# Four graph layers on one core: moving the inversion, the divisions and the output product of the attention heads

## The chip, the cores and the metric

The kernel runs on one core of a Trainium2 chip. The metric is the device time of one execution in microseconds. A core has five engines that each work through their own queue: TensorE (PE; its weight loads are listed as PEld), VectorE (DVE), ScalarE (ACT), GpSimd (POOL) and SyncE (SP), which here only issues DMAs.

## The reference

Eight graphs (batch B = 8) share one adjacency of N = 2048 nodes with about nine edges per node; every node has 64 features. Four layers follow one another, each with `x = layernorm(x + layer(x))`:

- layer 0: one-head attention with scores `leaky_relu(s1 + s2)`
- layer 1: a softmax over neighbours, feature by feature
- layer 2: the mean over neighbours, two products, relu and a layer norm
- layer 3: four heads of dot-product attention, an output product and a second dot-product attention:

```python
h = einsum('bnc,hdc->bhnd', x, Wh)                    # 4 heads
s = where(mask, einsum('...nd,...md->...nm', h, h), NEG)
out_h = einsum('...nm,...md->...nd', softmax(s), h) + bh
z = leaky_relu(concat of the heads of out_h, 0.2)     # [B, N, 256]
h2 = z @ Wo.T                                         # [B, N, 64]
out2 = the same attention on h2, + bo; leaky_relu; layer norm
```

The change lies in the heads of layer 3, from `h` to `h2`.

## The kernel before

**Stages in the profiled execution.** Layer 0 and the building of the edge lists end at about 445 us, layer 1 at about 700, layer 2 at about 920. The heads run from there to about 1450 us, the second attention from there to the end.

**Tiles of the heads.** The nodes are cut into NT = 16 node tiles of 128. The neighbours of a tile are gathered by list: two groups of 64 nodes, five windows each, so ten gathers of 128 rows (`xs` from the DRAM table `xtab`, `fetch`, L1080). GpSimd issues them, eight ahead, into ten buffers. Two gathers make a step `j`, five steps (0 to 4) a node tile. In each step TensorE does the following for all 8 graphs and 4 heads:

- `score` (L1093), twice: the scores of gathered rows against the tile's own side `U`. ScalarE takes the exponential (L1104), VectorE multiplies by the edges (L1107, "the mask").
- `turn` (L1085): transposes the rows of the next step; ScalarE copies them out (L1088).
- a "quarter" (`QUARTERS`, L1288): a piece of work for another tile.
- `back` (L1109), twice: sums of weighted rows into PSUM (`po`, two buffers). A block of 32 nodes that is complete is copied by VectorE into `os[it]` (L1130, tile name `o`, one buffer). Row 0 of each half of `o` holds the softmax denominators.

A node tile has four such blocks, closed in steps 1, 2, 3 and 4.

**What follows the sums.** The denominators are not divided by at once. After the last block they go through DRAM: SP stores the two rows to `dtab` (L1134) and loads them as `dT` (L1136). `invert` (L1139) takes the reciprocal, stores it to `itab` (L1143), checks it (L1144, L1145), and has SP load it, broadcast to 64 partitions each, as `R` (L1150, four DMAs of 256 KB, one buffer). Meanwhile `through_w` (L1167) multiplies `o` by the head's weights: TensorE L1064, ScalarE's copy L1171, VectorE's leaky relu L1172, into `z` (two buffers). `divide` (L1174) multiplies `z` by `R` (L1176), twice. `wo_all` (L1178) is the product with Wo (L1186), copied to `hT` (L1189) and stored to `utab`. `turn_back` (L1192) transposes `hT` into `h2` (L1196), and `with_bo` (L1199) adds the bias and stores to `ktab`. `top_pieces` and `low_pieces` (L1240, L1248) split `h2` into three bf16 pieces, stored to `ptab`, and add a bias to `X`.

**Order.** Within the heads the order on TensorE, ScalarE, VectorE and GpSimd is the program's order. Only SP's is left to a scheduler. The tables at L1288 to L1290 place the work of other tiles into the steps. The second entry is the offset of the tile, so `(invert, -1)` in step 2 of tile `it` inverts the sums of tile `it - 1`:

```python
QUARTERS = [(through_w, -1, 0), (through_w, -1, 2), (sides, 1, 0), (sides, 1, 2), (wo_all, -1)]
TURNED = {0: (turn_back, -2), 2: (turn_nodes, 2)}
FIRST = {1: [(top_pieces, -2)], 2: [(invert, -1)], 3: [(low_pieces, -2)], 4: [(divide, -1, 0), (divide, -1, 2)]}
```

`TURNED` and then `FIRST` stand ahead of the step's scores; the quarter stands between turn and back. GpSimd does the additions of `with_bo` and `low_pieces` inside the loop. The last tile doesn't take the way through DRAM: `last_invert` (L1153) and the lines after the loop (L1331 on) finish it.

Of the kernel before, what the change touches and what calls it, by code (L numbers as in the profile page):

```python
# [21 lines left out]
F32 = mybir.dt.float32  # L22
# [6 lines left out]
ALU = mybir.AluOpType  # L29
# [3 lines left out]
P = 128  # L33
# [15 lines left out]
def kernel(ctx: ExitStack, tc: tile.TileContext, ins: dict, out: bass.AP):  # L49
# [644 lines left out]
    RD = 2 * HN * NP  # L694
    recT = f3w.tile([RD, P], F32, name="recT")
    few = f3w.tile([RD, NT], F32, name="few")
    early = ExitStack()
# [345 lines left out]
    with early, ExitStack() as heads:  # L1043
# [48 lines left out]
        def score(k):  # L1092
# [14 lines left out]
            nc.vector.scalar_tensor_tensor(wt, wt, 3.0e38, edge, op0=ALU.min, op1=ALU.mult)  # L1107

        def back(k):  # L1109
            it, g, s = steps[k]  # L1110
# [15 lines left out]
            for blk, a, b in blocks_of(s):  # L1126
                if s == CLOSE[blk]:
                    if (g, blk) == (0, 0):
                        os[it] = wk.tile([P, HN, NP, P], F32, name="o", bufs=1)
                    nc.vector.tensor_copy(os[it][:, :, :, node_block(g, blk)].rearrange("p h a i -> p a h i"), pos.pop((it, g, blk)))  # L1130
            if (g, s) == (NG - 1, TURN[-1]) and it < NT - 1:
                rows_of = dtab[it].rearrange("(k n) i -> k (n i)", k=2)
                for k_ in range(2):
                    nc.sync.dma_start(rows_of[k_:k_ + 1], os[it][k_ * D:k_ * D + 1].rearrange("p h a i -> p (h a i)"))  # L1134
                dTs[it] = wk.tile([2 * HN * NP, P], F32, name="dT")
                nc.sync.dma_start(dTs[it], dtab[it])  # L1136

# [77 lines left out]
        def add_head(it, h, ph):  # L1215
# [6 lines left out]
            else:  # L1222
# [4 lines left out]
                for k in range(2):  # L1227
                    nc.vector.tensor_tensor(h2[:, HB + 1 - k::2], so_far[:, HB + k::2], dst[:, HB + k::2], ALU.add)
                with_bo(it, nc.vector)

# [16 lines left out]

        def low_pieces(it, eng=nc.gpsimd):  # L1248
            hp3, rest = in_pieces.pop(it)
            nc.scalar.copy(hp3[:, 1], rest)  # L1250
            eng.tensor_tensor(hp3[:, 2], rest, hp3[:, 1], ALU.subtract)
            nc.sync.dma_start(ptab[it * P:(it + 1) * P, :], hp3.rearrange("p k n -> p (k n)"))
            eng.tensor_tensor(X[:, it], X[:, it], over(b3, [P, B, D]), ALU.add)

# [32 lines left out]

        QUARTERS = [(through_w, -1, 0), (through_w, -1, 2), (sides, 1, 0), (sides, 1, 2), (wo_all, -1)]  # L1288
        TURNED = {0: (turn_back, -2), 2: (turn_nodes, 2)}
        FIRST = {1: [(top_pieces, -2)], 2: [(invert, -1)], 3: [(low_pieces, -2)], 4: [(divide, -1, 0), (divide, -1, 2)]}  # L1290
        PER = NG * GS // 2

        engines = {mybir.EngineType.PE, mybir.EngineType.Activation, mybir.EngineType.DVE, mybir.EngineType.Pool}
        AHEAD = 8
        with tc.manual_schedule(engines=engines):
            def call(of, f, t, *a):
                if 0 <= of + t < (NT if t > 0 else NT - 1):
                    f(of + t, *a)
# [8 lines left out]
            for m in range(len(steps) // 2):  # L1307
# [22 lines left out]

            t = NT - 1  # L1331
            through_w(t, 0)
            through_w(t, 2)
# [7 lines left out]
            for it in (t - 1, t):  # L1341
                top_pieces(it)
                low_pieces(it, nc.vector)

    with ExitStack() as fifth:
# [181 lines left out]
        def look():  # L1527
            many_recs(8, last_recs)
            nc.vector.memset(nbad[:, 9:10], 0.0)
            nc.vector.tensor_reduce(nbad[0:RD, 9:10], few[:, 0:NT - 1], AX.X, ALU.add)  # L1530
            nc.vector.tensor_scalar(nbad[0:RD, 9:10], nbad[0:RD, 9:10], float((NT - 1) * P), None, op0=ALU.not_equal)
            lack = fp.tile([P, 5, NT], F32, name="lack")
# [624 lines left out]
```

## Time and profile before

| what | us |
|---|---|
| median of 3 runs | 1844.16 |
| lowest and highest of them | 1836.62, 1847.84 |
| the profiled execution | 1753.84 |
| its span, first to last instruction | 1752.0 |
| TensorE busy in the span | 1326.0 (76%) |
| VectorE busy | 1219.1 (70%) |
| ScalarE busy | 910.7 (52%) |
| GpSimd busy | 830.5 (47%) |
| mean granted TensorE clock | 0.870 |

How to read it: all durations below come from the one profiled execution, which took less than the timed runs. A line of a profile names the source line, the engine, the operation, and the tiles as out<-in. A bracket at the end of a line is the engine's idle time just before, and what ended it. The clock is the share of TensorE's full clock that was granted. Busy time of an engine that isn't the bound of its stage costs nothing.

### The profile page before, as it was taken

The numbers are of one execution on the slowest core, as the hardware profiler recorded it, in microseconds if no ns is written. First come the engines' busy times: TensorE is split into PE (matmuls) and PEld (weight loads), VectorE is DVE, ScalarE is ACT, GpSimd is POOL, SyncE is SP. The second block draws the span as 40 slices with busy tenths as digits, with TensorE's granted clock in tenths as the row PEclk, the third lists the DMA queues.
The fourth block names the chain that finished last, engine by engine and source line by source line (L and its number), as shares of the span: only waits on it lengthen the run. The fifth ranks groups of instructions, "written<-read, shape, count | busy, mean of one in ns | idle before, by whom it ended". The sixth has DMA issues, their size and how long they took to land.

```text
span 1752.0 us, 39984 instructions
## 1 busy us (share of the span) xinstructions
PE 1326.0 (76%) x16028; PEld 923.5 (53%) x16028; DVE 1219.1 (70%) x2931; ACT 910.7 (52%) x1863; POOL 830.5 (47%) x820
## 2 busy tenths in 40 slices
PE   4674355552689996898947878889789787999993
PEld 3663233321233332732217767777677675888783
DVE  5889479897676465665774666766667654787787
ACT  5763234645951232535654546555556443477674
POOL 0000576670564652666625334434444316677761
PEclk9755567776799998999878999999999997999997
DMA  6451566661226883256614565654645527687771
GB/s 186 167 168 49 158 203 192 190 200 33 92 99 217 320 309 127 86 158 187 188 52 136 134 160 145 156 155 135 161 135 144 155 73 239 181 235 214 216 213 45
DMA packets 154139, 280.71 MB, mean 160 GB/s; under 512 B 64892, under 2 KB 91452, under 8 KB 151868
## 3 DMA queue, kind: packets, MB, share of 16 engines
q0 software_dynamic: 56320, 189.44, 36.2%
q1 hardware_dynamic: 80986, 84.45, 16.3%
q10 hardware_dynamic: 16640, 4.20, 1.1%
q8 instruction: 128, 2.10, 0.5%
q14 instruction: 65, 0.53, 0.1%
HBM read 237.60 MB, written 40.42 MB: 159 GB/s over the span
## 4 chain that ended last, share of the span: by engine, by line
PE 30%; DVE 15%; DMA 10%; ACT 7%; issue 4%; POOL 2%; SPq 2%; DVEq 0%; ACTq 0%; POOLq 0%
DMA R<-itab 6%; PE pa L605 6%; PE pscore L1101 3%; PE po L1123 3%; PE pa L660 3%; PE ps L1413 2%; DVE w L1107 2%; PE pscore L1186 2%; DMA itab<-rT 2%; PE po L1452 2%; PE py L833 2%; SPq L1150 2%; PE pt L1390 1%; PE pa L1003 1%; ACT z L870 1%
## 5 line engine op out<-in xcount | busy, mean ns | idle before, releaser
L204 POOL DMA_INDIRECT xs<-xtab,src x160 | 166.3, 1039 | 269.7 <-PE po L1123 238.2
L204 POOL DMA_INDIRECT hs<-htab,src x160 | 153.7, 960 | 240.4 <-PE pe L455 181.8
L1107 DVE SCALAR_TENSOR_TENSOR w<-w,Sel 128x640 f32<-128x640 f32 (+2 forms) x160 | 174.3, 1125 | 83.9 <-ACT w L1104 83.7
L605 PE MATMUL pa<-R,ET 128*128 128x512 bf16 x768 | 179.9, 391 | 50.3 <-POOL R L593 34.7
L1104 ACT ACTIVATE w<-pscore 128x640 f32<-128x640 f32 (+2 forms) x160 | 119.4, 747 | 135.4 <-PE pscore L1101 128.1
L204 POOL DMA_INDIRECT hs<-ktab,src x160 | 158.0, 987 | 60.6 <-issue 36.3
L1101 PE MATMUL pscore<-U,xsT 64*128 64x80 f32 (+2 forms) x2560 | 161.9, 277 | 1.1 <-ACT xsT L1088 1.1
L170 ACT ACTIVATE X<-X,ln_m,ln_r 128x64 f32<-128x64 f32 x256 | 87.2, 428 | 144.7 <-DVE ln_m L162 144.7
L605 PEld LDWEIGHTS <-ET 128*128 128x128 fp8e4 x768 | 74.8, 100 | 163.3 <-issue 83.5
L1123 PE MATMUL po<-w,xs 128*64 128x88 f32 (+2 forms) x3072 | 131.0, 239 | 31.3 <-DVE w L1107 30.1
L1101 PEld LDWEIGHTS pscore<-U,xsT 64*128 64x128 f32 x2560 | 150.9, 190 | 5.5 <-ACT xsT L1088 1.3
L1123 PEld LDWEIGHTS po<-w,xs 128*64 128x64 f32 x3072 | 114.5, 141 | 69.8 <-DVE w L1107 58.7
L204 POOL DMA_INDIRECT rs<-rtab,src x80 | 76.1, 951 | 62.5 <-PE pa L660 42.8
L614 DVE RECIPROCAL rec<-pa 128x256 f32<-128x256 f32 x32 | 54.1, 1730 | 64.2 <-PE pa L660 38.0
L1413 PE MATMUL ps<-U,hsT 128*128 128x64 f32 x768 | 95.5, 271 | 1.5 <-ACT hsT L1391 1.5
L1413 PEld LDWEIGHTS ps<-U,hsT 128*128 128x128 f32 x768 | 94.2, 195 | 1.9 <-ACT hsT L1391 1.7
L476 DVE TENSOR_TENSOR hs<-hs,w 128x1024 f32<-128x1024 f32 x80 | 91.8, 1214 | 3.3 <-ACT w L465 3.3
L1500 ACT ACTIVATE z<-z,ln_m,ln_r 128x64 f32<-128x64 f32 x240 | 83.5, 431 | 15.4 <-DVE ln_m L1488 15.4
L1003 PE MATMUL pa<-Y,ET 128*128 128x512 bf16 x384 | 90.1, 384 | 0.0
L204 POOL DMA_INDIRECT rs<-ytab,src x80 | 77.4, 968 | 24.0 <-issue 15.3
L1088 ACT COPY xsT<-pt 128x1024 f32<-128x1024 f32 x80 | 80.5, 1007 | 10.0 <-PE pt L713 9.9
L1452 PE MATMUL po<-hs,w 128*32 128x65 f32 x2048 | 72.9, 225 | 7.7 <-DVE w L1425 7.7
(637 smaller groups left out, 3029.5 us busy)
## 6 DMA issues: line engine op xcount, KB each, us to landing
at<-in_adj SPq DMA_DIRECT2D x16, 1024.0 KB
R<-itab SPq DMA_DIRECT2D x60, 256.0 KB
rtab<-r SPq DMA_DIRECT2D x16, 512.0 KB
ptab<-hp SPq DMA_DIRECT2D x16, 384.0 KB
hi<-ptab SPq DMA_DIRECT2D x16, 384.0 KB
ktab<-hb SPq DMA_DIRECT2D x16, 260.0 KB
X<-in_x ACTq DMA_DIRECT2D x16, 256.0 KB
htab<-H SPq DMA_DIRECT2D x16, 256.0 KB
```

The lines of the kernel that those rows point to most:

```text
L170: nc.scalar.activation(v[:, b], v[:, b], AF.Identity, scale=rstd[:, k:k + 1], bias=nmr[:, k:k + 1])
L204: nc.gpsimd.indirect_dma_start(out=dst, out_offset=None, in_=table[:, :], in_offset=bass.IndirectOffsetOnAxis(ap=src[:, it, s, g:g + 1], a ...
L476: nc.vector.tensor_tensor(wx, wx, along(w[:, own].rearrange("p g b -> p (g b)")), ALU.mult)
L605: nc.tensor.matmul(po[h].rearrange("p a f -> p (a f)"), ET[:, jt, it * P:(it + 1) * P], R[:, jt, q, h].rearrange("p a f -> p (a f)"), star ...
L1003: nc.tensor.matmul(sums[it], ET[:, jt, it * P:(it + 1) * P], Y[:, jt, q].rearrange("p a n -> p (a n)"), start=(jt == 0 and q == 0), stop=( ...
L1101: nc.tensor.matmul(pscore[:, k_, f0:f0 + HN * ni].rearrange("p (h i) -> p h i", i=ni), xsT[half, p], Us[it][half, p, :, i0:i0 + ni], start ...
L1104: nc.scalar.activation(w.rearrange("p k a h i -> p k (a h i)"), pscore[:, :, 0:NP * HN * ni], AF.Exp)
L1107: nc.vector.scalar_tensor_tensor(wt, wt, 3.0e38, edge, op0=ALU.min, op1=ALU.mult)
L1123: nc.tensor.matmul(po[half, p, :, a - blk * GB:b - blk * GB], xs[:, f0:f0 + D], w[:, k_, p, :, a - WINDOWS[s][0]:b - WINDOWS[s][0]], start ...
L1413: nc.tensor.matmul(pscore[:, g, 2 * p:2 * p + 2], hsT[:, g, p], U[:, p, :, node_block(g, k)], start=False, stop=(p == NP - 1))
L1452: nc.tensor.matmul(po[node_block(g, k), j, b], w[:, g, t], hs[:, g, t], start=(s == BEGIN[k] and b == 0), stop=(s == END[k] and b == B // ...
L1500: nc.scalar.activation(v, v, AF.Identity, scale=r, bias=n)
```

## The change

The work of the heads is placed anew, in four respects.

- **The inversion.** `dT`, `rT` and the check's tiles are 128 partitions x 32 instead of 32 x 128. The same 4096 numbers are read and stored row by row in DRAM order (`spread`). `invert` moves from ahead of step 2's scores to behind step 1's turn.
- **Divisions and Wo.** `divide` and `wo_all` move from step 4 of the next tile to step 0 of the tile after that. What precedes and follows shifts by a step: `through_w` to steps 1 and 2, `turn_back` to 1, `top_pieces` to 2, `turn_nodes` to 3, `low_pieces` to 4, `sides` to 3 and 4. After the loop, the divisions and Wo of tile 14 are added.
- **GpSimd.** The additions of `with_bo` and `low_pieces` run on VectorE. `with_bo` reads the PSUM tile of the transposes instead of `h2`. `low_pieces` gives its ScalarE copy to a new `middle_piece`, behind step 3's turn.
- **First block's copy.** The copy of the first block of sums into `o` moves from step 1's back to behind step 2's turn (`out_of_sums`).

```diff
-    recT = f3w.tile([RD, P], F32, name="recT")
-    few = f3w.tile([RD, NT], F32, name="few")
+    recT = f3w.tile([P, RD], F32, name="recT")
+    few = f3w.tile([P, NT], F32, name="few")
...
+        def out_of_sums(it, g, blk):
+            nc.vector.tensor_copy(os[it][:, :, :, node_block(g, blk)].rearrange("p h a i -> p a h i"), pos.pop((it, g, blk)))
...
                     if (g, blk) == (0, 0):
                         os[it] = wk.tile([P, HN, NP, P], F32, name="o", bufs=1)
-                    nc.vector.tensor_copy(os[it][:, :, :, node_block(g, blk)].rearrange("p h a i -> p a h i"), pos.pop((it, g, blk)))
+                    if (g, blk) != (0, 0):
+                        out_of_sums(it, g, blk)
...
-                dTs[it] = wk.tile([2 * HN * NP, P], F32, name="dT")
-                nc.sync.dma_start(dTs[it], dtab[it])
+                dTs[it] = wk.tile([P, RD], F32, name="dT")
+                nc.sync.dma_start(dTs[it], spread(dtab[it]))
+
+        def spread(rows_of):
+            return rows_of.rearrange("r i -> (r i)").rearrange("(p c) -> p c", c=RD)
...
-            rT = wk.tile([RD, P], F32, name="rT")
+            rT = wk.tile([P, RD], F32, name="rT")
             nc.vector.reciprocal(rT, dT)
-            nc.sync.dma_start(itab[it], rT)
+            nc.sync.dma_start(spread(itab[it]), rT)
...
-            with_bo(it, nc.gpsimd)
-
-        def with_bo(it, eng):
+            with_bo(it, ph[:, :, 0].rearrange("p k a d -> p a k d"))
+
+        def with_bo(it, v):
             hb = hbs[it % 2]
-            eng.tensor_tensor(hb[:, :, 1:1 + P].rearrange("p a (k d) -> p a k d", d=D), h2s[it].rearrange("p (a k) d -> p a k d", k=2),
-                              over(bo, [P, NP, 2, D]), ALU.add)
+            nc.vector.tensor_tensor(hb[:, :, 1:1 + P].rearrange("p a (k d) -> p a k d", d=D), v, over(bo, [P, NP, 2, D]), ALU.add)
...
-        def low_pieces(it, eng=nc.gpsimd):
+        def middle_piece(it):
+            hp3, rest = in_pieces[it]
+            nc.scalar.copy(hp3[:, 1], rest)
+
+        def low_pieces(it):
             hp3, rest = in_pieces.pop(it)
-            nc.scalar.copy(hp3[:, 1], rest)
-            eng.tensor_tensor(hp3[:, 2], rest, hp3[:, 1], ALU.subtract)
+            nc.vector.tensor_tensor(hp3[:, 2], rest, hp3[:, 1], ALU.subtract)
             nc.sync.dma_start(ptab[it * P:(it + 1) * P, :], hp3.rearrange("p k n -> p (k n)"))
-            eng.tensor_tensor(X[:, it], X[:, it], over(b3, [P, B, D]), ALU.add)
+            nc.vector.tensor_tensor(X[:, it], X[:, it], over(b3, [P, B, D]), ALU.add)
...
-        QUARTERS = [(through_w, -1, 0), (through_w, -1, 2), (sides, 1, 0), (sides, 1, 2), (wo_all, -1)]
-        TURNED = {0: (turn_back, -2), 2: (turn_nodes, 2)}
-        FIRST = {1: [(top_pieces, -2)], 2: [(invert, -1)], 3: [(low_pieces, -2)], 4: [(divide, -1, 0), (divide, -1, 2)]}
+        QUARTERS = [(wo_all, -2), (through_w, -1, 0), (through_w, -1, 2), (sides, 1, 0), (sides, 1, 2)]
+        TURNED = {1: (turn_back, -2), 3: (turn_nodes, 2)}
+        BEFORE = {0: [(divide, -2, 0), (divide, -2, 2)], 2: [(top_pieces, -2)], 4: [(low_pieces, -2)]}
+        BEHIND = {1: [(invert, -1)], 2: [(out_of_sums, 0, 0, 0)], 3: [(middle_piece, -2)]}
...
-                for of in FIRST.get(j, ()):
+                for of in BEFORE.get(j, ()):
                     call(it, *of)
                 for k in two:
                     score(k)
                 if 2 * m + 2 < len(steps):
                     turn((2 * m + 2, 2 * m + 3))
+                for of in BEHIND.get(j, ()):
+                    call(it, *of)
                 call(it, *QUARTERS[j])
...
             t = NT - 1
+            divide(t - 1, 0)
+            divide(t - 1, 2)
+            wo_all(t - 1)
             through_w(t, 0)
             through_w(t, 2)
```

The remaining lines fit the check of the inverted sums at the end of the kernel to the new shape.

More of the change, by code (lines that the diff above doesn't have):

```diff
@@ L1228, in add_head @@
                     nc.vector.tensor_tensor(h2[:, HB + 1 - k::2], so_far[:, HB + k::2], dst[:, HB + k::2], ALU.add)
-                with_bo(it, nc.vector)
+                with_bo(it, h2.rearrange("p (a k) d -> p a k d", k=2))
         def turn_last(it):
@@ L1296, in call @@
             def call(of, f, t, *a):
-                if 0 <= of + t < (NT if t > 0 else NT - 1):
+                if 0 <= of + t < (NT if t >= 0 else NT - 1):
                     f(of + t, *a)
@@ L1342 @@
                 top_pieces(it)
-                low_pieces(it, nc.vector)
+                middle_piece(it)
+                low_pieces(it)
     with ExitStack() as fifth:
@@ L1528, in look @@
             many_recs(8, last_recs)
-            nc.vector.memset(nbad[:, 9:10], 0.0)
-            nc.vector.tensor_reduce(nbad[0:RD, 9:10], few[:, 0:NT - 1], AX.X, ALU.add)
-            nc.vector.tensor_scalar(nbad[0:RD, 9:10], nbad[0:RD, 9:10], float((NT - 1) * P), None, op0=ALU.not_equal)
+            nc.vector.tensor_reduce(nbad[:, 9:10], few[:, 0:NT - 1], AX.X, ALU.add)
+            nc.vector.tensor_scalar(nbad[:, 9:10], nbad[:, 9:10], float((NT - 1) * RD), None, op0=ALU.not_equal)
             lack = fp.tile([P, 5, NT], F32, name="lack")
```

## The prediction

> **What bounds the kernel now.** I read the page's chain of work first, because a change in one stage can only pay there.
>
> ```profile
> PE 30%; DVE 15%; DMA 10%; ACT 7%; issue 4%; POOL 2%; SPq 2%; DVEq 0%; ACTq 0%; POOLq 0%
> DMA R<-itab 6%; PE pa L605 6%; PE pscore L1101 3%; PE po L1123 3%; PE pa L660 3%; PE ps L1413 2%; DVE w L1107 2%; PE pscore L1186 2%; DMA itab<-rT 2%; PE po L1452 2%; PE py L833 2%; SPq L1150 2%; PE pt L1390 1%; PE pa L1003 1%; ACT z L870 1%
> ```
>
> The load of the inverted sums, `R<-itab`, its store and its issue make 10% of the chain, and all three belong to the heads. Next come the waits inside the heads (window 970 to 1420 us; us in total, times, longest), first TensorE's, then VectorE's.
>
> ```profile
> PE pscore L1186 <- DVE z L1176: 33.8, 13, 4.5
> PE po L1123 <- DVE w L1107: 28.4, 39, 1.7
> ...
> DVE w L1107 <- ACT w L1104: 56.1, 42, 1.7
> DVE z L1176 <- DMA R<-itab: 40.1, 14, 4.8
> ```
>
> TensorE waits for two things: for the divided `z` before Wo (L1186), which waits for R, and for the masks (L1107). Third, the timeline of TensorE in part of one node tile shows where these waits stand.
>
> ```profile
> 1099.68 2.02 PE L1101 MATMUL pscore<-U,xsT 64*128 64x96 f32 x32
> 1101.54 0.66 PE L713 MATMUL pt<-ident,xs 64*128 64x64 f32 x16
> 1102.12 1.09 PE L1064 MATMUL pscore<-xT,G 64*64 64x256 f32 x16
> 1104.87 1.76 PE L1123 MATMUL po<-w,xs 128*64 128x48 f32 x48 [1.65 <-DVE w L1107]
> 1106.56 2.02 PE L1101 MATMUL pscore<-U,xsT 64*128 64x80 f32 x32
> 1108.42 0.66 PE L713 MATMUL pt<-ident,xs 64*128 64x64 f32 x16
> 1110.59 1.71 PE L1186 MATMUL pscore<-z,WoT 64*64 64x256 f32 x24 [1.51 <-DVE z L1176]
> ```
>
> Apart from these two waits TensorE runs without a gap: it is the bound, and the waits are what can be won. Fourth, why the masks are late, in the same timeline and in a tile where GpSimd has finished.
>
> ```profile
> 1070.76 1.17 POOL L1251 TENSOR_TENSOR hp<-rest,hp 128x512 bf16<-128x512 f32 x1
> 1070.86 3.91 DVE L1107 SCALAR_TENSOR_TENSOR w<-w,Sel 128x768 f32<-128x768 f32 x2 [1.58 <-ACT w L1104]
> 1071.88 1.27 POOL L1253 TENSOR_TENSOR X<-X,b 128x512 f32<-128x512 f32 x1
> ...
> 1421.94 1.76 DVE L1107 SCALAR_TENSOR_TENSOR w<-w,Sel 128x768 f32<-128x768 f32 x2 [1.90 <-ACT w L1104]
> ```
>
> The same two masks take 3.91 us beside GpSimd's two operations and 1.76 us without. Last, two node tiles by windows (from one L1142 to the next; length, busy time of PE, PEld, DVE, ACT, POOL, then clock, DMA share, GB/s), and all fourteen together.
>
> ```profile
> 1095.88:1126.32 30.44, 26.75 (x548) 22.45 (x548) 21.88 (x27) 17.83 (x25) 14.30 (x14) 1.00 0.57 155
> 1254.94:1289.74 34.80, 28.84 (x548) 23.85 (x548) 21.88 (x26) 17.83 (x25) 14.30 (x14) 0.90 0.53 136
> 967.21:1416.11 448.90, 385.37 (x7610) 321.82 (x7610) 303.04 (x352) 248.31 (x336) 191.86 (x177) 0.97 0.55 146
> ```
>
> The first tile waited 1.85 us for R, the second 4.12 us. It is 4.36 us longer for 2.27 us more of waiting: the clock fell after the wait, and TensorE's work took 28.84 instead of 26.75 us. The mean tile is 448.90 / 14 = 32.06 us.
>
> **What the skill says.** "SBUF — State Buffer", section "Who interferes with whom": a VectorE instruction with two SBUF inputs contends with a GpSimd instruction that reads SBUF, and the second to issue blocks. The mask has two SBUF inputs; the 3.91 against 1.76 us agree. "TensorE: Matmul & The Clock Gate", Part 1: TensorE falls to half clock after an idle window of about 3.4 us. The trace agrees in kind: each wait of 3.5 to 4.9 us for R is followed by a 5 us stretch at 0.50 to 0.82, while most waits near 2 us leave 1.00. "VectorE: DVE Perf Modes", section "Why PSUM operands drop a tier": PSUM input limits fp32 to one element a cycle. For an fp32 `tensor_tensor` the trace shows no difference: 691 ns from PSUM (L1217) and 683 ns from SBUF (L1253 on VectorE). "DMA: Bandwidth & Descriptors", Specifications: under 512 B the DMA engine does a read-modify-write; the change makes the rows of dT and itab 128 B. No run here shows such a pair.
>
> **Part by part, for one node tile.** A clean step on TensorE is scores 2.0, turn about 0.5 after overlap, a quarter 1.1 and back 1.4 to 1.75 us. VectorE's two masks end about 3.8 us after the step's scores begin.
>
> *Inversion.* `reciprocal` on 32 x 128 takes 930 ns. The 128 x 256 one (L614) takes 1730, so 800 ns more for 128 more elements, 6.25 ns each; 32 elements then cost about 930 - 96 x 6.25 = 330 ns. The two checks fall from 215 and 280 to an estimated 115 and 180. VectorE gets about 0.8 us back. The group also moves from ahead of step 2's masks to behind step 1's; the 0.20 us that TensorE waits in step 2 goes. Its input: dT is issued 3.5 us after the tile's first scores (1087.29 against 1083.77), and the inversion falls due at about 6.4 + 0.4 + 3.8 = 10.6 us, so the trip has 7 us. The itab store of the same size took 2.2 to 3.5 us on the chain. Doubling it for 128 B rows still fits: cost 0, at the other end 0.5 us.
>
> *Division and Wo.* In the fourteen full tiles R let the divisions start 12.2 to 14.7 us after the reciprocal's end. From 11 us after the new tile's start to the divisions 0.8 us into the next tile are some 17 us. So the wait for R goes, with SP's issue of the four loads and the ptab store behind them no longer near anyone. What is late next: the divisions (2 x 1.22 us) stand ahead of step 0's masks and behind the last copy of sums, 0.1 to 0.8 us. They end at 3.2 us. Wo's first half may start at 2.5, when turn ends, and needs the first `z` (2.0); its second half starts at 3.6. The masks end at 4.05 and 5.0 us; back starts at 4.7, and its second part at 5.3. Cost 0; 0.4 us if the queue slips. Their old cover was R itself, so nothing is lost in step 4.
>
> *GpSimd's arithmetic.* Three operations of 1.29, 1.17 and 1.27 us leave GpSimd; three of 0.69 us join VectorE. The masks win back 3.91 - 1.76 = 2.15 us and 2.68 - 1.62 = 1.06 us. VectorE's sum: 21.88 - 3.2 - 0.8 + 2.1 = 20.0 us in a tile of 27: not the bound. TensorE's 1.65 us goes, and about 0.3 us of step 0. `with_bo` now reads the transposes' PSUM buffer, which the next turn needs 2 us later: ready at about 1.3, cost 0. The subtraction and the addition before step 4's masks delay the first of them by 0.3 us, which the quarter hides.
>
> *First copy of sums.* It leaves step 1 and stands behind step 2's masks. The single buffer `o` is still read by `through_w` there, which ends 3.6 us into the step; the copy (0.68 us) then ends at about 4.5. Back's second part needs the PSUM buffer that it frees and could start at 4.25. Cost 0.3 to 0.4 us; ends 0 and 1.2 (if VectorE comes late from the leaky step, which ends 0.7 us into step 2, and the top piece behind it).
>
> *The tail.* Wo and the divisions of tile 14 now run after the loop: `through_w` starts about 3.4 us later after the last back, and 2.14 + 1.25 us leave step 4. Cost 0, between -2 and 2.
>
> *Sum.* 30.44 - 1.65 - 1.51 - 0.3 - 0.2 = 26.8, which is TensorE's busy 26.75; with 0.4 of the copy and 0.2 for slips 27.4 us. That is 4.66 below the mean tile: 3.0 are the clean tile's and 1.6 the longer waits and the clock's. 14 x 4.66 = 65, and the last tile's mask wait of 1.5 us may go too, which I leave as reserve. The ends: 27.0 us gives 71, 28.8 us gives 46. The profiled execution took 1753.84 us (span 1752.0), so 1689. The median of the runs shown is 1844.16, 90 us above it, and no view says where these lie. I carry the difference over as it is: 1844 - 65 = 1779. If the heads stretch with the rest the gain rises 5%, to 68; if their TensorE work is slower, R waits less and the gain falls towards 50.
>
> **Rivals.**
> *VectorE's queue becomes the limit.* For: the slack ahead of the masks is 0.1 to 0.6 us in steps 0, 2 and 4. Against: 20 us busy in 27. At 0.4 us more in each of five steps the tile is 29.4: 14 x 2.66 = 37, so 1807.
> *The relief doesn't come.* R is late again by about 2 us, because its 1 MB meets the gathers (the DMA share already stands at 1.0 there) in a shorter tile. Against: 3 us of slack. TensorE's wait for z returns in step 0 and holds the masks too: about 31 us a tile, 14 x 1 = 14, so 1830.
> *Slower: the trip of the sums.* dtab's write and dT's 128 B reads take 12 us instead of 7. Then the reciprocal blocks VectorE with leaky, the top piece, step 2's masks and the copy behind it, and TensorE idles about 4.5 us; with the clock's 2.1 us that is 6.6 against 4.66 gained: 14 x 1.94 = 27, so 1871. It decides from 2.6 us of gap (7 + 0.5 + 2.6, about 10 us of trip). Against: 16 KB only, and no sign of a wait for dT today.
>
> **How the numbers follow.** The forecast has 0.64 (own range 1768 to 1798), VectorE 0.18, no relief 0.08, slower 0.10. A measurement here tells about 1% from no change. Forecast and VectorE give faster by over 1%, 0.82; no relief gives within 1%, 0.08; the last 0.10 slower. The range reaches from 1762 (71 us and the 5%, with the last tile's reserve) to 1822, which takes in VectorE's case.
>
> **What would show it.** No DVE wait for R in the heads; L1107's 768-wide pair near 1.8 us everywhere; tiles of 27 to 28 us at clock 1.00; R's DMA gone from the chain. TensorE waits of over 1 us behind the copy of sums or the divisions point to the VectorE rival, a wait of the reciprocal on dT to the slower one. A tile above 31 us makes the forecast wrong.

## The result and the profile after

| comparison | kernel before | changed kernel | ratio, 95% interval |
|---|---|---|---|
| of the result | 1846.0 us (4 runs) | 1815.9 us (4 runs) | 0.9847, 0.9801 to 0.9894 |
| again, group B | 1848.6 us (17 runs) | 1831.7 us (5 runs) | 0.9914, 0.9897 to 0.9930 |
| again, group A | 1746.6 us (11 runs) | 1678.2 us (6 runs) | 0.9601, 0.9568 to 0.9634 |

The change is faster, by 30 us where 65 were forecast. The kernels of one comparison ran on the same chip, and the comparisons fall into two groups by the time of the kernel before: about 1750 us (A below) and about 1848 us (B). The profile that the prediction read, 1753.84 us, is of group A; the times it was to be held against are of group B. The later comparisons ran on five chips, two that gave A and three that gave B; none was met twice, and that of the result isn't on record. So whether A and B are kinds of chips or conditions that one chip can be in isn't shown. The changed kernel gains 68 us in A and 17 and 30 us in B.

The changed kernel in the comparison of the result (span 1808.8 us, group B), the page's chain of work:

```profile
PE 48%; ACT 8%; DVE 7%; issue 5%; DMA 1%; another core or an unknown queue 1%; POOL 1%; SPq 0%; ACTq 0%; POOLq 0%; DVEq 0%
PE pscore L1101 9%; PE pa L605 6%; PE po L1126 5%; PE ps L1429 5%; PE po L1468 4%; PE pt L1406 3%; PE pa L660 2%; PE pt L713 2%; ACT w L1104 2%; PE pa L1003 2%; PE pscore L1064 2%; PE py L833 2%; PE pe L1399 2%; PE pscore L1193 2%; ACT xsT L1088 1%
```

DMA went from 10% of the chain to 1%: R's load, store and issue are gone from it. The waits inside the heads (window 980 to 1440 us; us in total, times, longest):

```profile
PE pscore L1064 <- ACT w L1104: 13.3, 32, 0.6
PE po L1126 <- ACT z L1178: 5.0, 10, 0.5
...
PE pscore L1193 <- DVE z L1183: 2.0, 1, 2.0
```

TensorE no longer waits for the divided `z`, except once behind the loop, and its waits for the masks have shrunk to 2.6 us in 4 (longest 1.1). What is left are many small waits for ScalarE, which head the list here and don't appear in the list that the prediction read (in group B the kernel before has them too, see below). Next, all fourteen intervals between reciprocals (length, busy time of PE, PEld, DVE, ACT, POOL, clock, DMA share, GB/s): the changed kernel of the result, then the changed kernel in A, the kernel before in A and the kernel before in B.

```profile
998.60:1408.50 409.90, 380.54 (x7612) 319.22 (x7611) 278.33 (x392) 242.35 (x336) 151.78 (x138) 1.00 0.61 160
```

```profile
962.90:1337.40 374.50, 368.31 (x7614) 314.51 (x7614) 279.76 (x392) 248.25 (x336) 154.38 (x138) 1.00 0.67 175
```

```profile
965.80:1415.60 449.80, 386.55 (x7614) 322.67 (x7610) 302.79 (x353) 248.40 (x336) 191.08 (x177) 0.97 0.55 146
```

```profile
1012.70:1456.20 443.50, 394.54 (x7604) 327.61 (x7604) 272.36 (x352) 242.17 (x336) 185.14 (x177) 0.97 0.57 148
```

Divided by 14, a tile of the changed kernel takes 29.28 us in the result's run and 26.75 in A; a tile of the kernel before 32.13 in A and 31.68 in B. The tiles of the kernel before lose nothing when it goes from A to B; those of the changed kernel lose 2.5 us each (3.2 in the other run in B). Of these 2.5 us, 1.7 are idle time of TensorE and 0.9 recorded busy time (27.2 for 26.3 us a tile); the single matmuls are recorded as equally long (scores 275 ns in both), and the granted clock is 1.00 in both. The whole heads, from the first gather of `xs` to the first gather of the fifth stage, in us:

| | before, A | changed, A | before, B | changed, B (result) | changed, B (again) |
|---|---|---|---|---|---|
| to the first reciprocal | 44.1 | 41.7 | 53.4 | 50.6 | 52.4 |
| 14 tiles | 449.8 | 374.5 | 443.5 | 409.9 | 419.4 |
| from the last reciprocal | 35.2 | 37.8 | 34.9 | 39.0 | 40.7 |
| heads | 529.1 | 454.0 | 531.8 | 499.5 | 512.5 |
| fifth stage, to the end | 302.0 | 298.9 | 364.8 | 361.3 | 359.6 |

The reciprocal itself moved: it starts 9.7 us after its tile's first scores in the changed kernel in A, and 11.9 before. So some 2 us pass from the first row to the last without being won or lost. Counted from the last tile's first scores, the end of the heads takes 47.3 us before and 47.6 after in A, and 47.3, 48.8 and 51.0 in B.

The spans of the kernel before differ by 103 us between the groups: 26 to the last gather of layer 0, 11 from there to the heads, 3 in the heads and 63 in the fifth stage. Outside the heads the changed kernel differs by much the same (23 to 26, 4 to 9 and 61 to 62 us), so none of that is the change's.

### The profile page after: what moved, and what is told of

It is laid out like the page before. It is cut to its first block, busy times and chain, and to the rows that moved or that the text cites. A ratio compares the mean times of both kernels' runs of the same rounds, so it can differ in the third digit from the quotient of the medians.

```text
span 1808.8 us, 39940 instructions
## 1 busy us (share of the span) xinstructions
PE 1378.3 (76%) x16028; PEld 949.9 (53%) x16028; DVE 1195.8 (66%) x2973; ACT 905.6 (50%) x1863; POOL 782.8 (43%) x777
## 4 chain that ended last, share of the span: by engine, by line
PE 48%; ACT 8%; DVE 7%; issue 5%; DMA 1%; another core or an unknown queue 1%; POOL 1%; SPq 0%; ACTq 0%; POOLq 0%; DVEq 0%
PE pscore L1101 9%; PE pa L605 6%; PE po L1126 5%; PE ps L1429 5%; PE po L1468 4%; PE pt L1406 3%; PE pa L660 2%; PE pt L713 2%; ACT w L1104 2%; PE pa L1003 2%; PE pscore L1064 2%; PE py L833 2%; PE pe L1399 2%; PE pscore L1193 2%; ACT xsT L1088 1%
## 5 line engine op out<-in xcount | busy, mean ns | idle before, releaser
L204 POOL DMA_INDIRECT xs<-xtab,src x160 | 172.9, 1081 | 282.0 <-PE po L1126 243.9
L1107 DVE SCALAR_TENSOR_TENSOR w<-w,Sel 128x640 f32<-128x640 f32 (+2 forms) x160 | 134.2, 875 | 104.7 <-ACT w L1104 104.5
L1104 ACT ACTIVATE w<-pscore 128x640 f32<-128x640 f32 (+2 forms) x160 | 113.6, 745 | 145.5 <-PE pscore L1101 139.9
L1468 PE MATMUL po<-hs,w 128*32 128x65 f32 x2048 | 87.3, 234 | 33.2 <-issue 25.3
L1429 PE MATMUL ps<-U,hsT 128*128 128x64 f32 x768 | 104.3, 287 | 9.0 <-ACT hsT L1407 4.8
L1429 PEld LDWEIGHTS ps<-U,hsT 128*128 128x128 f32 x768 | 102.8, 210 | 10.0 <-ACT hsT L1407 5.4
L1468 PEld LDWEIGHTS po<-hs,w 128*32 128x32 f32 x2048 | 70.8, 118 | 45.0 <-issue 33.4
L1407 ACT COPY hsT<-pt 128x512 f32<-128x512 f32 x96 | 52.5, 586 | 81.8 <-remote 46.4
```

The source lines that it names most:

```text
L204: nc.gpsimd.indirect_dma_start(out=dst, out_offset=None, in_=table[:, :], in_offset=bass.IndirectOffsetOnAxis(ap=src[:, it, s, g:g + 1], a ...
L1104: nc.scalar.activation(w.rearrange("p k a h i -> p k (a h i)"), pscore[:, :, 0:NP * HN * ni], AF.Exp)
L1429: nc.tensor.matmul(pscore[:, g, 2 * p:2 * p + 2], hsT[:, g, p], U[:, p, :, node_block(g, k)], start=False, stop=(p == NP - 1))
L1468: nc.tensor.matmul(po[node_block(g, k), j, b], w[:, g, t], hs[:, g, t], start=(s == BEGIN[k] and b == 0), stop=(s == END[k] and b == B // ...
```

## The experiments

Below, a tile is the mean of the fourteen intervals between reciprocals. Two theories were held against each other. *V*: VectorE's arithmetic ahead of the masks (top_pieces in step 2, low_pieces in step 4) holds up exponentials and masks. *T*: TensorE is later than its records show.

**The kernel before, three more times.** No edit.

> The kernel before, unchanged, for a second profile. The first profiled execution (1753.84 us) lies 92 us under the median of its timed runs (1846), and in it layer 0 took 445 us against 466 after and the fifth stage 297 against 358, in code that the change doesn't touch. If that is the execution and not the kernel, this profile spans about 1840 us, with layer 0 near 465 and the fifth stage near 350, and the heads from the first gather to the first gather of the fifth stage at 528 us as before. If the change has lengthened the other stages, layer 0 and the fifth stage are again near 445 and 297.

> The kernel before, for its profile beside the run of the changed kernel on the same chip. Where it takes about 1848: theory T expects TensorE's semaphores late against its recorded ends there too (in some 40% of the updates in the heads, as in the three kernels profiled so), a tile of about 32 us, since the waits for R give TensorE time to catch up, layer 0 near 466 and the fifth stage near 355. Where it takes about 1750: as in the second profile, 32.1 a tile, layer 0 at 444, the fifth stage at 301, no late semaphores.

> The kernel before, for a profile where it takes about 1848 us. Theory T (TensorE's late updates cost every kernel there, and the waits for R hide part of them in the kernel before): updates late in 30 to 45% of the cases in its heads too, but the step that waits for R no longer than elsewhere; a tile of 31.5 to 33 us, so that the change gains 2 us a tile there and not 5; layer 0 near 466 us and the fifth stage near 355. If the late updates belonged to the order of the changed kernel: no late updates in its heads. Where it takes about 1750: as in the profiles before, 31.9 to 32.1 a tile.

The first two met group A: 1755.96 and 1754.57 us, tiles of 32.31 and 32.13 us, layer 0 and the fifth stage as in the first profile. The third met group B: 1857.7 us, a tile of 31.68 us. So the long layer 0 and fifth stage belong to the group and not to the change. The waits of the kernel before in A (window 990 to 1400 us), TensorE's and VectorE's:

```profile
PE pscore L1186 <- DVE z L1176: 29.4, 12, 4.1
PE po L1123 <- DVE w L1107: 26.3, 36, 1.7
...
DVE z L1176 <- DMA R<-itab: 35.2, 13, 4.4
```

and in B (window 1030 to 1440 us):

```profile
PE pscore L1064 <- ACT w L1104: 13.4, 34, 0.6
PE pt L713 <- issue: 11.5, 43, 0.5
PE po L1123 <- DVE w L1107: 6.2, 13, 0.7
PE pscore L1186 <- DVE z L1176: 5.6, 5, 1.5
...
DVE z L1176 <- DMA R<-itab: 9.7, 6, 2.5
```

This is the core of the case. In thirteen tiles VectorE waited 35.2 us for R in A, and 9.7 us in B; TensorE waited 29.4 us for the divided `z` in A, and 5.6 us in B. The waits that the change removes were for the most part not there in B. They were covered by a longer way to them: from scores to scores, in the mean of fourteen tiles, steps 0, 2 and 3 were 0.4, 0.5 and 0.4 us longer in B, step 4 was 1.7 us shorter (7.91 for 9.58). In their place stand waits for ScalarE's exponentials, and 11.5 us of short gaps before turns for which the profile names nothing ("issue").

**The changed kernel, twice more.** No edit.

> The changed kernel, unchanged, a second time. With its pieces moved behind the masks it ran at 1687 us beside a kernel before of 1751, and the result of 1816 stood beside a kernel before of 1846: the two comparisons had different times for the same kernel before. Theory C (what was 92 us longer in the comparison of the result is that run's condition, the same for both kernels in kind and not caused by the change): where the kernel before takes about 1750 us here, layer 0 takes 445 us again, a tile of heads 27.2 to 27.6 and the whole 1685 to 1695, a ratio of 0.963 to 0.968. Theory V (the pieces ahead of the masks are what cost the missing 2 us a tile): a tile of 28.5 to 29.3, the whole 1705 to 1718, a ratio of 0.974 to 0.981, whatever the condition.

> The changed kernel, unchanged, a third time, for the missing pair: so far it was only timed where the kernel before takes 1846 to 1849 us (there a tile of heads of 29.3 and 30.0 us), and the forecast rests on a profile of the kernel before at 1754. Where the kernel before takes about 1750: theory T (what the kernels lose where the kernel before takes 1846 is TensorE's, whose semaphores there come later than the ends in its records) expects a tile of 27.2 to 27.6 us, the whole at 1685 to 1695, a ratio of 0.963 to 0.968; theory V (the pieces ahead of the masks) a tile of 28.5 or more, 1705 or more. Where the kernel before takes about 1848 again: a tile of 29.3 to 30.1 and a ratio of 0.983 to 0.992 by both.

The first met B: 1831.7 us and 29.96 us a tile. Theory V was to hold there too, at 28.5 to 29.3 and a ratio of 0.974 to 0.981; it got 0.9914. The second met A: 1678.2 us, a ratio of 0.9601 and 26.75 us a tile, with nine of fifteen tiles, from scores to scores, at 26.53 to 26.58 us. That is theory T's side, and somewhat better than its 27.2 to 27.6. TensorE's waits in A (window 980 to 1320 us) are

```profile
PE pscore L1101 <- issue: 0.9, 1, 0.9
PE po L1126 <- issue: 0.8, 1, 0.8
```

and nothing else: it runs through, busy 368.31 of 374.50 us. Where B differs is seen in the timeline of step 2 of one tile, first in A, then in B (start, length, engine; in brackets the idle time before):

```profile
1097.86 2.02 PE L1101 MATMUL pscore<-U,xsT 64*128 64x88 f32 x32
...
1099.04 1.59 ACT L1104 ACTIVATE w<-pscore 128x704 f32<-128x704 f32 x2 [0.82 <-PE pscore L1101]
...
1100.30 1.09 PE L1064 MATMUL pscore<-o,AT 64*64 64x256 f32 x16
```

```profile
1158.32 2.02 PE L1101 MATMUL pscore<-U,xsT 64*128 64x88 f32 x32
...
1161.00 1.35 ACT L1104 ACTIVATE w<-pscore 128x704 f32<-128x704 f32 x2 [2.18 <-PE pscore L1101]
1161.79 0.89 DVE L1107 SCALAR_TENSOR_TENSOR w<-w,Sel 128x704 f32<-128x704 f32 x1 [1.62 <-ACT w L1104]
1161.81 0.88 PE L1064 MATMUL pscore<-o,AT 64*64 64x256 f32 x12 [0.46 <-ACT w L1104]
```

The scores have the same recorded length, 2.02 us. The first exponential starts 1.18 us after them in A and 2.68 us after them in B, where ScalarE stood idle for 2.18 us. The quarter's matmuls need the buffer that the exponential reads; they start 2.44 us after the scores in A and 3.49 in B. What ScalarE waited for is TensorE's semaphore, the counter by which one engine's result releases another engine. The Trainium skill, "Perfetto Trace Analysis", section "Tensor Engine Instruction (MATMUL, LD_WEIGHTS)", says that TensorE's end in a profile is estimated, and that the semaphore update comes when PSUM has acknowledged the writes. The trace has both, and here they part. Worked out from the semaphore events, update minus recorded end, in us:

```
step 2, changed kernel     14 tiles, A   14 tiles, B (again)
scores, first half             0.02        1.50 to 1.72
scores, second half            0.02        0.77 to 1.00
next turn                  0.01 to 0.02    0.01 to 0.20
quarter                        0.04            0.04

updates over 0.15 us late, in the fourteen tiles
A: before 0 of 444, changed 0 of 445
B: before 41%, changed 42% (result) and 43% (again)
```

In the result's run the first half's update is 1.40 to 1.73 us late in ten of fourteen tiles and about 0.75 in the other four. VectorE's and ScalarE's updates are on time in both groups (medians 0.01 us, none over 0.15), and their durations are the same (the 704-wide mask 891 ns in A, 889 in B). The gathers are no slower either: one of their packets takes 159 ns in the median in both. So it is TensorE's, and it is of the group and not of the change. It is not simply a slower array: in B an update that was 1.5 us late is followed by the next, of 16 further matmuls, 0.16 us later in most tiles (0.89 in A), and the one after that is nearly on time. What holds these updates back stays open. All nine profiles of A have no late update in the tiles, all eleven of B have 37 to 45%. Nor is it peculiar to the heads: in the three profiles of B above, 13% of TensorE's updates are late in layer 0 and 18 to 59% in the later stages, in A at most three of some 1180 in the whole program. In the waits of the fifth stage the profile has a name of its own for a semaphore that comes long after the recorded end (changed kernel in B, window 1468 to 1827 us):

```profile
ACT hsT L1407 <- remote: 42.5, 9, 5.6
...
ACT w L1432 <- remote: 27.7, 12, 10.6
```

In A neither line appears.

**The pieces behind the masks.**

```diff
-BEFORE = {0: [...], 2: [(top_pieces, -2)], 4: [(low_pieces, -2)]}
-BEHIND = {1: [(invert, -1)], 2: [(out_of_sums, 0, 0, 0)], 3: [(middle_piece, -2)]}
+BEFORE = {0: [...]}
+BEHIND = {1: [(invert, -1)], 2: [(out_of_sums, 0, 0, 0), (top_pieces, -2)], 3: [(middle_piece, -2)], 4: [(low_pieces, -2)]}
```

> The changed kernel, with top_pieces and low_pieces called behind the masks and the next turn (in BEHIND) and no longer ahead of the scores of steps 2 and 4. In the changed kernel a tile of heads takes 29.28 us where 27.4 was forecast, and steps 2 and 4 are each about 1 us too long; in just these steps the first exponentials begin 2 to 2.5 us after the first score and 0.2 us after the end of rest or of X + b3. Theory V (VectorE's arithmetic ahead of the masks holds up the exponentials and masks): the tile falls to about 27.5 us, the total by about 25 us to 1791. Theory T (TensorE's own work is longer than its records show, and the exponentials are late because the scores are): nothing moves, tile 29.0 to 29.5, total within 5 us of 1816.

> The changed kernel with top_pieces and low_pieces behind the masks, again. Where the kernel before takes 1848, theory T: TensorE is the floor there, the tile stays at 29.3 to 30.1 us and the whole within 8 us of the changed kernel's. Theory V: 27.5 to 28.5 and some 25 us less than the changed kernel. Where the kernel before takes 1750: 27.2 and 1687 again, and the difference to the changed kernel beside it is what the place of the pieces is worth: theory T within 6 us, theory V 20 to 30.

Both met A: 1687.2 and 1686.1 us (ratios 0.9643, 0.9598 to 0.9689, and 0.9651, 0.9610 to 0.9693), tiles of 27.44 and 27.41 us. When the first came in it looked like a success of theory V, since only the 29.28 of group B was known; beside the changed kernel in A (26.75) it is 0.66 us a tile worse. Its one repeated TensorE wait says why (window 1000 to 1330 us):

```profile
PE pscore L1101 <- DVE U L1074: 8.4, 11, 0.8
```

Behind step 4's masks, low_pieces delays the copy of U, for which the next tile's scores wait 0.8 us. Theory V fell in A: ahead of the masks is the better place there. This kernel was not met in B.

**Bfloat16 in the quarters.** The operands are read as the upper halves of the float32 values.

```diff
-nc.tensor.matmul(pq[to, j, n]..., W[own, h, own], v(h)[own, 2 * j:2 * j + 2]..., ...)
+nc.tensor.matmul(pq[to, j, n]..., W[own, h, own].bitcast(BF16)[:, 1::2], v(h)[own, 2 * j:2 * j + 2]....bitcast(BF16)[:, 1::2], ...)
```

> The changed kernel, with the matmuls of quarters (sides and through_w, 64 of a tile's about 550) reading the upper halves of their float32 operands as bfloat16: the low bits are left out. The other engines' instructions are the same. The records give these matmuls 61.5 us in 14 tiles, 4.4 us a tile; [...] TensorE has about 3 us a tile less to do. Theory T: TensorE is the floor, and the tile falls by 2 to 3 us, to 26.3 to 27.3, the total to about 1780. Theory V: TensorE has room already; the tile stays above 28.7 us.

> The changed kernel with the operands of quarters read as the upper halves of their float32 values (the low bits are left out), again: about 3 us a tile less for TensorE, nothing less for the others. Where the kernel before takes 1848, theory T: the tile falls from 30.0 to 26.5 to 28 us. A limit that is not TensorE's execution (instructions arriving, VectorE, DMA): 29 us or more. Where the kernel before takes 1750: 25.65 and 1666 again; the difference to the changed kernel beside it says how far TensorE is the floor there: 1.5 us or more a tile if the changed kernel is at 27.2, 3 or more if it is at 28.7.

> The changed kernel with the operands of quarters read as the upper halves of their float32 values (the low bits are left out). On the other chip it took 25.65 us a tile for 26.53. Where the kernel before takes 1848: if the late updates are TensorE working off more than it can, less work makes them fewer and the tile falls by 1 us or more from 30.0, to 29 or less; if they come late whatever it has to do, the tile stays between 29.3 and 30.1. Where the kernel before takes 1750: 25.7 again.

In A twice: 1665.8 and 1668.6 us (0.9531 and 0.9547), tiles of 25.81 and 25.89 us. A quarter before (as of the changed kernel in A) and after, both from the timeline of TensorE:

```profile
1095.53 1.09 PE L1064 MATMUL pscore<-o,AT 64*64 64x256 f32 x16
1096.55 1.38 PE L1126 MATMUL po<-w,xs 128*64 128x88 f32 x32
```

```profile
1098.83 0.42 PE L1064 MATMUL pscore<-o,AT 64*64 64x256 bf16 x8
1099.31 0.83 PE L1126 MATMUL po<-w,xs 128*64 128x88 f32 x16
1100.76 0.78 PE L1126 MATMUL po<-w,xs 128*64 128x80 f32 x16 [0.63 <-DVE o L1110]
```

From the quarter's start to the start of back it is 1.02 us in float32 and 0.48 in bfloat16 (half of the bfloat16 records are missing, so starts are compared and not busy times): 0.54 us less in each of four quarters, 2.2 us a tile where about 3 were expected. The tile fell by 0.9 only. TensorE was the floor in A, but by less than 1 us: with less to do it waits for masks and for the copy of sums (8.4 and 7.5 us in a window of 320 us). In B: 1826.6 us (0.9839, 0.9792 to 0.9886), a tile of 29.43 us for 29.96, but after the first tile ten of fourteen lie between 27.5 and 29.3 and three at 31.4 to 31.8 us. Each of these three has a stretch of 6.8 us at half the clock (0.89 in the window of the tile), the others have none. Updates over 0.15 us late fell from 43% to 37%. A microsecond was asked for and half of one came in the mean, but 1.2 in the eleven tiles at full clock (28.7 us after the first tile, for 29.9 in the changed kernel). This leaves undecided how far the late updates depend on TensorE's load.

**GpSimd's additions back on GpSimd**, in the places of the change.

```diff
-            with_bo(it, ph[:, :, 0].rearrange("p k a d -> p a k d"))
+            with_bo(it, h2s[it].rearrange("p (a k) d -> p a k d", k=2), nc.gpsimd)
-            nc.vector.tensor_tensor(hp3[:, 2], rest, hp3[:, 1], ALU.subtract)
-            nc.vector.tensor_tensor(X[:, it], X[:, it], over(b3, [P, B, D]), ALU.add)
+            nc.gpsimd.tensor_tensor(...)   # both
```

> The changed kernel, with the three additions that it took from GpSimd (h2 + bo, the third piece, X + b3) back on GpSimd, h2 + bo reading the copy in SBUF; the places in the order are those of the change. Theory V: VectorE has 2 us a tile less ahead of its masks but the masks beside GpSimd's additions take longer again, 2.15 us for steps 1 and 4 by the profile before: tile between 28.3 and 29.8 us. Theory T: the masks have room, tile 29.0 to 29.6, total within 6 us of 1816. The prediction's own sum (shorter masks are worth about a microsecond and more a tile): tile 30.3 or more, total about 1831.

In A: 1705.2 us (0.9747, 0.9700 to 0.9794), a tile of 28.76 us. Against the changed kernel in A that is 2.0 us a tile, or 28 us of the change's 75 in the heads; some 6 of the 28 lie in two tiles with a stretch of low clock, and the most frequent tile is 28.38 us for 26.53. The masks in this kernel (window 990 to 1350 us), then in the changed kernel in A (980 to 1320 us); columns: busy, mean ns, idle before:

```profile
L1107 DVE SCALAR_TENSOR_TENSOR w<-w,Sel 128x640 f32<-128x640 f32 x50 | 67.9, 1358 | 12.4 <-ACT w L1104 12.4
L1107 DVE SCALAR_TENSOR_TENSOR w<-w,Sel 128x704 f32<-128x704 f32 x51 | 52.2, 1024 | 51.7 <-ACT w L1104 51.7
```

```profile
L1107 DVE SCALAR_TENSOR_TENSOR w<-w,Sel 128x704 f32<-128x704 f32 x50 | 44.6, 891 | 9.5 <-ACT w L1104 8.9
L1107 DVE SCALAR_TENSOR_TENSOR w<-w,Sel 128x640 f32<-128x640 f32 x51 | 42.0, 823 | 1.0 <-ACT w L1104 0.9
...
L1107 DVE SCALAR_TENSOR_TENSOR w<-w,Sel 128x768 f32<-128x768 f32 x26 | 24.9, 956 | 12.1 <-ACT w L1104 12.1
```

The same masks take 1358 and 1024 ns in the mean with GpSimd's additions and 823 and 891 without, four of each kind in a tile: 2.7 us of VectorE's time. With R out of the way TensorE waits for masks again, 17.0 us in 12 waits, and step 4 is 1.3 us longer than the changed kernel's (6.47 for 5.13).

**One part at a time.** The inversion alone in the kernel before (tables spread over 128 partitions, as in the change's diff), three times:

```diff
-FIRST = {1: [(top_pieces, -2)], 2: [(invert, -1)], 3: ...
+FIRST = {1: [(top_pieces, -2)], 3: ...
+                if j == 1:
+                    call(it, invert, -1)      # behind score and turn
```

> The kernel before with the first part of the change alone: the sums inverted on 128 partitions, called behind step 1's masks and not ahead of step 2's scores; divisions, Wo and GpSimd's additions where they were. If R's trip is what holds the tile, an issue some 4 to 5 us sooner takes most of the long wait for R in step 4 (3.5 to 4.9 us) away: a tile of 28.5 to 30 us for 32.1. If the sums' trip to dT becomes late (the rival on the slower side), VectorE waits for dT in step 1 and the tile stays at 31 or more.

> The kernel before with the first part of the change alone (sums inverted on 128 partitions, behind step 1's masks). Where the kernel before takes 1848 it had 30.0 us a tile, as the whole change. Where it takes 1750: R some 5 us sooner; theory R (the wait for R is all that a tile loses, 3.5 to 4.9 us): 27.5 to 28.6 us a tile, a ratio of 0.966 to 0.975; if masks beside GpSimd's additions are the next limit, as the change with the additions back on GpSimd (28.38) suggests, 28.4 to 29.5.

> The kernel before with the first part alone (sums inverted on 128 partitions, behind step 1's masks), for the chip where the kernel before takes 1747 us. If the wait for R is all that a tile loses beside GpSimd's additions: 27.5 to 28.6 us a tile, a ratio of 0.966 to 0.975. If masks beside GpSimd's additions are the next limit, as the change with the additions back on GpSimd (28.38) suggests: 28.4 to 29.5. Where the kernel before takes 1848: 30.0 again.

The changed kernel with the inversion as it was, on 32 partitions (the expectations say 16, which is a slip) and in step 2, three times:

```diff
-BEFORE = {..., 2: [(top_pieces, -2)], ...}
-BEHIND = {1: [(invert, -1)], 2: ...}
+BEFORE = {..., 2: [(invert, -1), (top_pieces, -2)], ...}
+BEHIND = {2: ...}
```

> The changed kernel with the inversion as it was: on 16 partitions, reciprocal and checks of 930 + 215 + 280 ns, ahead of step 2's scores. Divisions and Wo stay in the next tile's step 0, so R has the time of steps 2, 3 and 4, some 16 us, for a trip that had about 13 before. R is not waited for; only VectorE's 0.8 us more remain, ahead of step 2's masks. If the moved division alone frees the path: a tile within 0.8 us of the changed kernel's on the same chip. If the inversion on 128 partitions is needed too: 1.5 us or more above it.

> The changed kernel with the inversion on 16 partitions and ahead of step 2's scores, as it was. Where the kernel before takes 1848 it had 30.0 us a tile, as the whole change. Where it takes 1750: if the moved divisions alone free the path, a tile of 26.5 to 27.3 us, within 0.8 us of the change; if the sooner inversion is needed too, 27.5 or more, and a wait for R in step 0.

> The changed kernel with the inversion on 16 partitions and ahead of step 2's scores, as it was, for the chip where the kernel before takes 1747 us. If the moved divisions alone free the path: a tile of 26.5 to 27.3 us, within 0.8 us of the change's 26.53. If the sooner inversion is needed too: 27.5 or more, and a wait for R in step 0. Where the kernel before takes 1848: 30.0 again.

GpSimd's additions alone in the kernel before:

```diff
-            with_bo(it, nc.gpsimd)
+            with_bo(it, ph[:, :, 0].rearrange("p k a d -> p a k d"))   # on VectorE
-        def low_pieces(it, eng=nc.gpsimd):
+        def low_pieces(it, eng=nc.vector):
```

> The kernel before with the third part alone: h2 + bo from PSUM, the third piece and X + b3 on VectorE, the inversion and the divisions where they were. The prediction's sum has the masks of steps 1 and 4 shorter by 2.15 and 1.06 us and three additions of 0.69 us on VectorE. While R ends step 4, a shorter mask of step 4 or an emptier VectorE is worth nothing there: a tile between 31.3 and 32.6 us, total within 10 us of the kernel before. If masks beside GpSimd set the pace by themselves: 30 to 31 us.

All seven ran in group B.

| group B | time | ratio, 95% interval | tile |
|---|---|---|---|
| inversion alone | 1831.0, 1829.4, 1828.7 us | 0.9905 (0.9882 to 0.9928), 0.9869 (0.9823 to 0.9915), 0.9885 (0.9830 to 0.9939) | 29.89, 29.99, 30.01 us |
| change with the old inversion | 1827.7, 1831.6, 1830.3 us | 0.9887 (0.9868 to 0.9907), 0.9873 (0.9828 to 0.9917), 0.9908 (0.9871 to 0.9945) | 29.81, 29.88, 29.86 us |
| GpSimd's additions alone | 1844.0 us | 0.9977 (0.9956 to 0.9997) | 31.31 us |
| the whole change, result | 1815.9 us | 0.9847 (0.9801 to 0.9894) | 29.28 us |
| the whole change, again | 1831.7 us | 0.9914 (0.9897 to 0.9930) | 29.96 us |

The sooner inversion alone frees the path from R, and so do the moved divisions (together with the change's other two parts): in neither does VectorE's list have a wait for R any more. Either brings about all of the gain there; the whole change had no more in one run and 0.5 to 0.7 us a tile more in the other. GpSimd's additions alone leave R in place (VectorE still waited 19.2 us for it in 11 waits) and bring almost nothing, as expected. The tiles without waits for R lie between 29.3 and 30.0 us in B, whichever part removed them. No part was run alone in A; how the 5.4 us of A divide over inversion and divisions stays open.

## Why the prediction was right in A and wrong in B

*What bounds the kernel* held in A, the group of its profile: TensorE runs without a gap once R and the masks are out of its way, and the floor was its busy time. The sum said 26.8 us and took 27.4 with 0.4 for the first copy and 0.2 for slips; measured were 26.75, so neither came. 14 tiles then gave 75.3 us in the profiles; the medians moved by 68.4 us, against 65 (68 where the prediction let the heads stretch). The lower end of its range, 1762, doesn't follow from its terms: 71 us, 5% and the reserve of 1.5 make 76, and 1768.

*The inversion*: `reciprocal` 330 ns forecast and 347 measured, the checks 115 and 180 against 182 and 192, VectorE's sum 20.0 against 279.76 / 14 = 20.0 us. R is waited for nowhere. The trip of the sums had 7 us by the sum and got 4.2 in the shorter tile (dT issued at 1065.89, reciprocal at 1070.11 us in A) without an idle VectorE before the reciprocal: the rival on the slower side has no trace.

*Division and Wo, first copy*: cost 0 and 0.3 to 0.4 us; in A neither left a wait on TensorE. *GpSimd's arithmetic*: the 768-wide masks fell to 956 ns each; the part is worth 2.0 us a tile in A, where the sum had 1.65 plus 0.3.

*The tail* was set at 0, between -2 and 2. From the end of the last sums to the fifth stage it cost 1.7 us in A and 3.2 and 4.9 in B; against it stands the last tile itself, shorter by 1.4 us in A and 1.6 and 1.1 in B, which the prediction had left as reserve. Behind the loop Wo waits for the divisions, which no other matmul covers any more. The wait and the start of Wo in A, from the waits (window 1337.4 to 1375.2 us) and the timeline:

```profile
PE pscore L1193 <- DVE z L1183: 2.0, 1, 2.0
```

```profile
1355.13 2.14 PE L1193 MATMUL pscore<-z,WoT 64*64 64x256 f32 x32 [2.02 <-DVE z L1183]
```

*The step that failed* is the size of the term that the change removes, 4.66 us a tile, carried over to runs that the profile doesn't stand for: "The median of the runs shown is 1844.16, 90 us above it, and no view says where these lie. I carry the difference over as it is". The 90 us were another condition and not a constant, and part of them lay in the heads in a form that the tile's length hid: late semaphores from TensorE in place of the wait for R. The prediction's own next sentence named the direction, "if their TensorE work is slower, R waits less and the gain falls towards 50"; it was too small. In place of 4.66 us, in B 1.7 to 2.4 were there to remove (31.68 less 29.96 and 29.28). 14 of these are 24 and 34 us; with the two ends the heads are 19 and 32 us shorter, beside 17 and 30 in the times. That the late updates are what takes the rest rests on what stands side by side: they are the one difference between the groups that was found in the traces, and no run switched them off. The stretches of low clock went with the waits for R, as forecast: 0.97 before, 1.00 after, in both groups. But they are not tied to these waits alone, as the three tiles in bfloat16 in B and two with the additions on GpSimd show, which don't wait for R; each of the two stretches begins 1.7 us after the end of a wait of 1.56 us for a mask, less than half of the 3.4 us that the prediction names.

The rival with VectorE's queue as the limit gave 29.4 us a tile and 1807 us, close to what B shows, but for another reason: TensorE waited little for VectorE there (9.1 us in 23 waits in the heads of the result's run, beside 2.0 behind the loop), and VectorE itself stood waiting 75.7 us for exponentials. A number that fits is not a mechanism that holds; in A, moving VectorE's pieces made the tile longer.

## What to carry to other kernels

When the profiled execution and the timed runs are 5% apart, they may be two conditions: find out which waits exist in the one that will be timed before pricing their removal, since a wait is only worth what isn't covered by another. A matmul's recorded end is a model; read TensorE's real pace from when its readers start (here the exponential 1.18 or 2.68 us after the same scores). Once the long wait is gone, look at what stands beside the bound engine: GpSimd's three additions cost 2.0 us a tile in the changed kernel (A) and 0.4 in the kernel before (31.68 to 31.31, B); the two were not measured in one group.

## What the runs showed of the hardware

In group B 37 to 45% of TensorE's semaphore updates in the heads' tiles came over 0.15 us after the recorded end, in a pattern tied to the place in the program (1.50 to 1.72 us at one place of all fourteen tiles of one run), while the recorded length of its matmuls, the granted clock (1.00 in the tiles of the changed kernel) and the other engines' durations look the same. 64x64 matmuls with 256 columns on every second bfloat16 of a float32 array took 0.48 us for sixteen, against 1.02 us in float32: a little less than half of the time.
